# VectorE's reads of kept numbers: an added zero in PSUM, a fixed place in VectorE's order, and a read at every step of the pass to the left

## The chip, the cores and the metric

The kernel runs on one core of one Trainium2 chip. The metric is device time in microseconds (us) from start to end; it is taken as the median of three runs. The core has a matrix engine (TensorE, PE in the profile), VectorE (DVE), ScalarE (ACT), GpSimd (POOL) and SyncE (SP, which issues the DMAs here). Each engine works through a queue of its own in order; an instruction that needs another engine's result waits for a semaphore, and all that is queued behind it on its engine waits too.

## The reference, cut to what matters

The input is `x` of (4, 48, 256, 256) in float32. Four layers follow each other, each `x = x + layer(groupnorm(x))`. Layers 0 and 1 (channel attention and a gated feed-forward) come before the part that is changed. Layers 2 and 3 are alike: recurrent scans over rows, then over columns, each step a five-tap convolution over 48 channels:

```python
def step(w, b):
    def f(carry, inp):
        nxt = inp + _conv1d(carry, w, b)
        return (nxt, nxt)
    return f
...
_, d_rest = jax.lax.scan(step(down_w, down_b), d0, xs[1:])
...
_, u_rest = jax.lax.scan(step(down_w, down_b), u0, seq)
...
_, r_rest = jax.lax.scan(step(right_w, right_b), r0, ws[1:])
...
_, l_rest = jax.lax.scan(step(left_w, left_b), l0, R[Ww - 2::-1])
```

So a layer has four passes, down, up, right and left, of 255 or 256 steps, and each step needs the one before it.

## The kernel before

Layers 2 and 3 are computed in `scans`. The batch of four is split into two chains, 0 and 1, of two images each; a chain goes through layer 2 and then layer 3. The 96 partitions hold 48 channels of even and of odd positions, so a step is two halves (one per image), each of three 96x96 matmuls over 128 positions into one PSUM bank. `step` (L1056) issues for each half the matmuls (L1064; the profile has two records for each float32 matmul, so 12 a step) and VectorE's addition of the PSUM sum and the step's input into the next `carry` (L1068 for down and up, where the input is a row, L1072 for right and left). There are `NC = 4` carry buffers, used in turn. After each addition, `keep` writes the step's result somewhere:

- down and up: ScalarE writes it over the row it came from (`dn`, L1150; `up`, L1194).
- right: ScalarE writes it to `lines` (L1286). The step's input is a column; GpSimd copies it from `col` to a small contiguous tile `pre` (`fetch`, L1259) `far` steps ahead. Chain 0 has three `pre` buffers and `far = 2`; chain 1 has four and `far = 3`.
- left: the input is a line of `lines`, and GpSimd adds the carry to `stage` (L1334), one addition for both halves. In layer 3 of chain 1 (`direct`) it adds each half into `done` (L1338), from where the output is written straight away.

Loads and stores of 1536 KB blocks go over SP's queue: a block is 16 steps in right and left.

An instruction of VectorE that must wait for two engines gets an extra instruction for the second wait. To keep such waits off the additions, VectorE reads now and then one number of what another engine wrote, into a tile `seen` that nobody uses: behind that read, VectorE knows that the other engine has come that far. `look` (L1030) does this in down, up and right: it keeps the place in a list, and reads the place kept three steps before. In right the same instruction reads a number of `pre` for the next step (`fetched`): a `tensor_add` of two SBUF numbers (L1041); otherwise it is a `tensor_copy` (L1039). In left, except in `direct`, a copy (L1348) at every second step reads the place kept two steps before.

A scheduler sets the order of each engine's queue from the program and from its own estimate of when operands are ready. It may place an instruction earlier or later than the program has it, so a `seen` read need not stand where the program asks for it.

The chains are started so that chain 0 goes alone for `LEAD = 992` steps, nearly the whole of its layer 2; then steps of the two chains alternate; then chain 1 does its layer 3 alone, while GpSimd also rearranges the output rows of chain 0 (`to_rows`, L1448). The start of chain 0 overlaps with the end of the gated layer. In left of layer 2, VectorE also takes statistics of the finished block with 8 `bn_stats` of 512 elements (L1376), one a step, for the next group norm.

Of the kernel before, what the change touches and what calls it, by code (L numbers as in the profile page):

```python
# [9 lines left out]
F32 = mybir.dt.float32  # L10
# [3 lines left out]
PSUM = bass.MemoryType.PSUM  # L14
DRAM = bass.MemoryType.DRAM

B, C, H, W = 4, 48, 256, 256
G = 16
NP = 2
P = 96  # L20
# [944 lines left out]
def scans(ctx, tc, xs, out, wts, biases, dram, k, coefs, lead, spare):  # L965
# [13 lines left out]
    nc = tc.nc  # L979
# [3 lines left out]
    pool = lambda name, bufs, **how: ctx.enter_context(  # L983
        tc.tile_pool(name=name, bufs=bufs, reuse_waits="tile", **how)
    )
# [6 lines left out]
    slots_d = pool("c_slot_d", 5)  # L992
    p_small = pool("c_ps", 1, space=PSUM)
    psum = pool("c_psum", 2, space=PSUM)
    sums = [spare, psum]
    buffers = [Ring([slots_a] * 3 + [slots_c, slots_b]), Ring([slots_d] * 5)]
    NT = H // RT
    NH = RT // 2
    CB = 2 * KC
# [16 lines left out]
    def take(pair, name):  # L1016
        return buffers[pair].tile([P, SLOT], F32, tag="slot", name=name)

    def chain(pair):
# [7 lines left out]
        seen = wp.tile([P, 1], F32, tag=f"seen{pair}", name="seen")  # L1027
        kept = []

        def look(place, fetched=None):  # L1030

            kept.append(place)
            if len(kept) > 3:
                if fetched is None:
                    nc.vector.tensor_copy(seen, kept.pop(0))  # L1039
                else:  # L1040
                    nc.vector.tensor_add(seen, kept.pop(0), fetched)  # L1041

        def slot(name):
            return take(pair, f"{name}{pair}")

        def inner():
            return carry[at[0]][:, :, 1 : HP - 1]
# [5 lines left out]
        def blocks(v):  # L1053
            return v.rearrange("p b (k w) -> p b k w", w=KC)
# [30 lines left out]
        def row(ts, r):  # L1085
            return rows_view(ts[r % 2])[:, :, :, r // 2, :]

        def load_rows(layer, n, r, t, k0, k1):

            v = rows_view(t)  # L1090
            for b in range(2):
                for q in range(2):
                    nc.sync.dma_start(
                        v[q * C : (q + 1) * C, b, k0:k1].rearrange("c k h w -> c k (h w)"),
                        xs[layer][pair][
                            r * C : (r + 1) * C, b, 2 * k0 + q : 2 * k1 - 1 + q : 2, n * NH : (n + 1) * NH, :
                        ].rearrange("c k h w -> c k (h w)"),
                    )

        def layer_of(layer, first):  # L1100
# [18 lines left out]
            def norm(t, b):  # L1119
                v = by_batch(t)[:, b]  # L1120
                g = biased[b]
                nc.scalar.activation(v, v, AF.Identity, bias=g[:, 1:2], scale=g[:, 0:1])
# [11 lines left out]
            for n in range(NT):  # L1134
                ahead_ = None
                for r in range(RT):
                    if r == 0:
                        kept.clear()
                        while len(halves) < min(2 * n + 5, 2 * NT):
                            t = slot("dn")  # L1140
                            load_rows(layer, len(halves) // 2, len(halves) % 2, t, 0, NK)
                            halves.append(t)
                        if n + 1 < NT:
                            ahead_ = halves[2 * n + 2 : 2 * n + 4]
                    if ahead_ and r in (11, 14, 22, 25):
                        norm(ahead_[r // 22], r % 11 // 3)
                    inp = row(now, r)

                    def keep(new, b):
                        nc.scalar.activation(inp[:, b], blocks(new[:, b]), AF.Identity, bias=bias[:, 0:1])  # L1150

                    if n == 0 and r == 0:
                        keep(inner(), slice(0, 2))
                    else:
                        step(layer, 0, inp, keep)
                    look(inp[:, 1, 0, 0:1])
                    yield
                if ahead_:
                    for r in range(2):
                        nc.sync.dma_start(D[n][r], now[r])  # L1160
                    now = ahead_
# [90 lines left out]
            fetched = {}  # L1252
# [59 lines left out]
            direct = layer == 1 and pair == NP - 1  # L1312
            done = None
            writes = []
            for n in reversed(range(NK)):
                ahead_ = None
                if direct and n % 2 == 1:
                    done = [take(0, "done") for _ in range(2)]
                for w in reversed(range(CB)):
                    if w == CB - 1 and n > 0:  # L1320
                        ahead_ = slot("lines"), slot("stage")
                        nc.sync.dma_start(ahead_[0], Rt[n - 1])
                        nc.sync.dma_start(by_batch(ahead_[1]), block_of(x, n - 1))
                    if layer == 0 and n == 0 and w == CB // 2:
                        following = [slot("dn"), slot("dn")]
                        for r in range(2):
                            load_rows(1, 0, r, following[r], 1, NK)
                    line = lines_view(lines)[:, w]
                    to = cols_view(stage)[:, :, w % 2, :, w // 2]

                    def keep(new, b):
                        if not direct:
                            if b.stop == 2:
                                nc.gpsimd.tensor_add(to, to, new)  # L1334
                            return
                        for i in range(b.start, b.stop):
                            place = done[i].rearrange("p (h w) -> p h w", w=2 * CB)[:, :, n % 2 * CB + w]
                            nc.gpsimd.tensor_add(place, to[:, i], new[:, i])  # L1338

                    if n == NK - 1 and w == CB - 1:  # L1340
                        keep(inner(), slice(0, 2))
                    else:
                        step(layer, 2, line, keep)
                    if not direct and w % 2:

                        kept.append(to[:, 1, H // 2 - 1 :])
                        if len(kept) > 1:
                            nc.vector.tensor_copy(seen, kept.pop(0))  # L1348
                    if late:
                        late.pop(0)()  # L1350
                    if writes and w % 8 == 4:
                        writes.pop(0)()
                    yield
                if layer == 0:
                    nc.sync.dma_start(block_of(y, n), by_batch(stage))
                elif not direct:
                    v = stage.rearrange("p (b q t n) -> p b q t n", b=2, q=2, t=NY)
                    for b in range(2):
                        for q in range(2):
                            nc.sync.dma_start(result[:, b, :, 2 * n + q], v[:, b, q])  # L1360
                elif n % 2 == 0:

                    def write(b, r, done=done, w0=n * CB):
                        at_rows = out[(2 * pair + b) * C : (2 * pair + b + 1) * C].rearrange(
                            "c (h r w) -> c h r w", r=2, w=W
                        )
                        nc.sync.dma_start(
                            at_rows[:, :, r, w0 : w0 + 2 * CB],
                            done[b][r * C : (r + 1) * C].rearrange("c (h w) -> c h w", w=2 * CB),
                        )  # L1370

                    writes += [lambda b=b, r=r, f=write: f(b, r) for b in range(2) for r in range(2)]
                if layer == 0:

                    def stat(b, c, n=n, v=by_batch(stage)):
                        nc.vector.bn_stats(stats[b][:, n * 4 + c, :], v[:, b, c * 512 : (c + 1) * 512])  # L1376

                    late += [lambda b=b, c=c, f=stat: f(b, c) for b in range(2) for c in range(4)]
                    if n == 0:
                        for r in range(2):  # L1380
                            for q in range(2):
                                nc.sync.dma_start(
                                    rows_view(following[r])[q * C : (q + 1) * C, :, 0].rearrange("c b h w -> c b (h w)"),
                                    cols_view(stage)[r * C : (r + 1) * C, :, q, :NH, :].rearrange("c b h w -> c b (h w)"),
                                )
                if ahead_:
                    lines, stage = ahead_
# [211 lines left out]
```

## Time and profile before

| | us |
|---|---|
| median of three runs | 9099.63 |
| the three runs | 9097.15 to 9100.62 |
| the profiled execution, its own time | 9105.24 |
| its span, first to last instruction | 9103.5 |
| PE busy | 8713.5 (96% of the span) |
| DVE busy | 3971.3 (44%) |
| ACT busy | 3440.2 (38%) |
| POOL busy | 1948.2 (21%) |
| scan matmuls, L1064: first start to last start | 3247.2 to 9070.5 |

The reads and additions on VectorE, by line, from the groups of instructions (line, engine, operation, out<-in, size, count, then busy us and mean ns of one, then idle time of the engine before them and what ended it):

```profile
L1072 DVE TENSOR_TENSOR carry<-ps,pre 96x128 f32<-96x128 f32 x2040 | 550.9, 284 | 271.1 <-PE ps L1064 239.7
...
L1041 DVE TENSOR_TENSOR seen<-lines,pre 96x1 f32<-96x1 f32 x1008 | 166.8, 165 | 479.6 <-POOL pre L1259 437.2
```

Where the chains are, by the first and last times of the lines: chain 0's down and up from 3247 to 4186, its right from 4186 to 4580, its left from 4580 to about 4980; both chains until about 7600; chain 1 alone after that, its last right from 8365 to 8715 and its last left from 8715 to 9071. A timeline line reads: start, duration, engine, line, operation, tiles, count, and in brackets how long the engine had been idle and who released it. A line of the table by stages reads: from and to, length, busy time and in brackets the number of records, the granted clock as a share of full speed, the busy share of the DMA engines, GB/s.

### The profile page before, as it was taken

What the parts mean: (1) busy time and instruction counts of PE and PEld (TensorE: products, weight loads), DVE (VectorE), ACT (ScalarE), POOL (GpSimd) and SP (SyncE); (2) the same over time, 40 slices, a digit from 0 to 9 for tenths busy, and PEclk for the clock granted to TensorE, in tenths of its full rate; (3) what the DMA queues carried; (4) which work ended last, traced back from release to release, by engine and by line L of the source; (5) the groups of instructions that cost most, each with busy time, mean ns of one, the idle gap of its engine ahead of it and who ended that gap; (6) DMA issues with size and microseconds to landing.
All of it is one profiled execution on the core that took longest, in us unless ns stands there. A gap on an engine that the chain in (4) does not pass through costs nothing. (4 is left out here: it accounts for less than half of the span.)

```text
span 9103.5 us, 158554 instructions
## 1 busy us (share of the span) xinstructions
PE 8713.5 (96%) x62920; PEld 7234.4 (79%) x62920; DVE 3971.3 (44%) x14031; ACT 3440.2 (38%) x7023; POOL 1948.2 (21%) x3100
## 2 busy tenths in 40 slices
PE   6999999999999978999999999999999999999998
PEld 4777777433333336999888999999999999999998
DVE  3232010234555555444345544444444555444543
ACT  0011000123343455765400776666554002765610
POOL 0000000001111120002444000001445664001566
PEclk9999999999999988999999999999999999999999
DMA  7664323467878877765466755465556787867789
GB/s 150 132 133 89 71 62 73 94 137 168 180 171 179 180 159 163 161 143 143 119 168 165 168 140 135 116 152 134 161 158 163 215 224 175 204 168 191 210 171 184
DMA packets 1180201, 1390.37 MB, mean 153 GB/s; under 512 B 263184, under 2 KB 1107216, under 8 KB 1118784
## 3 DMA queue, kind: packets, MB, share of 16 engines
q1 hardware_dynamic: 1179360, 1379.90, 64.9%
q8 instruction: 493, 8.08, 0.4%
q14 instruction: 252, 2.06, 0.1%
q0 software_dynamic: 96, 0.33, 0.0%
HBM read 811.21 MB, written 509.61 MB: 145 GB/s over the span
## 5 line engine op out<-in xcount | busy, mean ns | idle before, releaser
L1064 PE MATMUL ps<-carry,w 96*96 96x128 f32 x48960 | 5490.2, 274 | 115.0 <-DVE carry L1072 71.7
L1064 PEld LDWEIGHTS ps<-carry,w 96*96 96x96 f32 x48960 | 5407.4, 163 | 207.4 <-DVE carry L1072 134.7
L1259 POOL COPY pre<-col 96x256 f32<-96x256 f32 x1020 | 656.7, 644 | 2755.5 <-DMA col<-last 1971.7
L1150 ACT ACTIVATE dn<-carry,b 96x128 f32<-96x128 f32 (+1 forms) x2044 | 769.1, 398 | 838.3 <-DVE carry L1068 828.9
L1286 ACT ACTIVATE lines<-carry,b 96x128 f32<-96x128 f32 (+1 forms) x2044 | 780.2, 399 | 690.8 <-DVE carry L1072 650.1
L1068 DVE TENSOR_TENSOR carry<-ps,dn 96x128 f32<-96x128 f32 x2280 | 652.5, 287 | 755.8 <-PE ps L1064 730.5
L1194 ACT ACTIVATE up<-carry,b 96x128 f32<-96x128 f32 x1792 | 719.1, 402 | 459.8 <-DVE carry L1068 456.3
L1068 DVE TENSOR_TENSOR carry<-ps,up 96x128 f32<-96x128 f32 x1792 | 516.0, 288 | 598.9 <-PE ps L1064 594.1
L1334 POOL TENSOR_TENSOR stage<-stage,carry 96x256 f32<-96x256 f32 x768 | 656.2, 856 | 527.4 <-DVE carry L1072 497.5
L1072 DVE TENSOR_TENSOR carry<-ps,lines 96x128 f32<-96x128 f32 x2040 | 547.6, 283 | 424.9 <-PE ps L1064 401.1
L581 PE MATMUL py<-x1n,wy 128*96 128x512 f32 x1536 | 703.6, 607 | 30.4 <-ACT x1n L541 27.9
L1072 DVE TENSOR_TENSOR carry<-ps,pre 96x128 f32<-96x128 f32 x2040 | 550.9, 284 | 271.1 <-PE ps L1064 239.7
L295 PE MATMUL acc<-xs,xt 128*96 128x288 f32 x2048 | 666.7, 407 | 0.0
L294 PE MATMUL acc<-xt 128*96 128x288 f32 x2048 | 666.5, 409 | 0.0
L581 PEld LDWEIGHTS py<-x1n,wy 128*96 128x96 f32 x1536 | 245.2, 166 | 455.2 <-issue 437.0
L279 DVE COPY xt<-pt 128x384 f32<-128x384 f32 x256 | 136.6, 554 | 850.8 <-PE pt L276 650.3
L261 ACT ACTIVATE xn<-raw,coef 96x2048 f32<-96x2048 f32 x64 | 133.6, 2094 | 987.6 <-PE pt L276 819.6
L296 PE MATMUL acc<-xt,xs 128*96 128x192 f32 x2048 | 501.7, 327 | 0.0
L296 PEld LDWEIGHTS acc<-xt,xs 128*96 128x96 f32 x2048 | 332.1, 165 | 154.3 <-issue 1.4
L295 PEld LDWEIGHTS acc<-xs,xt 128*96 128x96 f32 x2048 | 332.0, 164 | 151.2 <-issue 2.2
L604 DVE TENSOR_TENSOR y<-py,t 96x512 f32<-96x512 f32 x256 | 171.4, 678 | 600.8 <-PE py L590 600.8
L1041 DVE TENSOR_TENSOR seen<-lines,pre 96x1 f32<-96x1 f32 x1008 | 166.8, 165 | 479.6 <-POOL pre L1259 437.2
(183 smaller groups left out, 5520.3 us busy)
## 6 DMA issues: line engine op xcount, KB each, us to landing
stage<-x SPq DMA_DIRECT2D x64, 1536.0 KB
dn<-x SPq DMA_DIRECT2D x240, 384.0 KB
R<-lines SPq DMA_DIRECT2D x60, 1536.0 KB
lines<-R SPq DMA_DIRECT2D x60, 1536.0 KB
D<-dn SPq DMA_DIRECT2D x56, 1536.0 KB
up<-D SPq DMA_DIRECT2D x56, 1536.0 KB
U<-up SPq DMA_DIRECT2D x224, 384.0 KB
col<-U SPq DMA_DIRECT2D x56, 1536.0 KB
```

Of the source, the lines that this page charges most:

```text
L294: nc.tensor.matmul(acc[0], lhsT=xt[:, h + 2, :], rhs=xt[:, here, :], start=first, stop=last)
L295: nc.tensor.matmul(acc[1], lhsT=xt[:, h + 2, :], rhs=xs[:, here, :], start=first, stop=last)
L296: nc.tensor.matmul(acc[2], lhsT=xs[:, h + 2, :], rhs=xt[:, past, :], start=first, stop=last)
L581: nc.tensor.matmul(ps, lhsT=held["w"][0][:, dx], rhs=x1n[:, 2 * c : 2 * c + 2, dx : dx + W], start=dx == 0, stop=False)
L1064: nc.tensor.matmul(ps, lhsT=w_sb[layer][:, way, j, :], rhs=old[:, i, j : j + W // 2], start=j == 0, stop=j == 2)
L1068: nc.vector.tensor_add(new[:, i].rearrange("p (k w) -> p k w", w=KC), ps.rearrange("p (k w) -> p k w", w=KC), inp[:, i])
L1072: nc.vector.tensor_add(new[:, i], ps, inp[:, i])
L1150: nc.scalar.activation(inp[:, b], blocks(new[:, b]), AF.Identity, bias=bias[:, 0:1])
L1194: nc.scalar.activation(place[:, b], blocks(new[:, b]), AF.Identity, bias=bias[:, 1:2])
L1259: nc.gpsimd.tensor_copy(t, cols_view(block)[:, :, w % 2, :, w // 2])
L1286: nc.scalar.activation(line[:, b], new[:, b], AF.Identity, bias=bias[:, 2:3])
L1334: nc.gpsimd.tensor_add(to, to, new)
```

## The change

A PSUM tile `zero` of one number per partition is allocated in `scans` and set to 0.0 by VectorE once. Every read is now a `tensor_add` of this zero and the number to be read. In right, the kept place and the fetched number are read by two instructions instead of one, and the fetched number is read at every step, also while the list is still short. Each read is pinned by `keep_in_program_order`: in VectorE's queue it stands behind the VectorE instruction that the program traced just before it, normally the step's second addition; it is not a wait. Later instructions may still be put ahead of it. Chain 0 leaves out the reads in the first 64 rows of down in layer 2. In left, `look` is called at every step and in `direct` too (on `done` there), and so reads the place kept three steps before.

```diff
+    p_zero = pool("c_zero", 1, space=PSUM)
     sums = [spare, psum]
+    zero = p_zero.tile([P, 1], F32, tag="zero", name="zero")
+    nc.vector.memset(zero, 0.0)
...
             kept.append(place)
-            if len(kept) > 3:
-                if fetched is None:
-                    nc.vector.tensor_copy(seen, kept.pop(0))
-                else:
-                    nc.vector.tensor_add(seen, kept.pop(0), fetched)
+            old = [kept.pop(0)] if len(kept) > 3 else []
+            for number in old + ([] if fetched is None else [fetched]):
+                tc.keep_in_program_order(nc.vector.tensor_add(seen, zero, number))
...
                         step(layer, 0, inp, keep)
-                    look(inp[:, 1, 0, 0:1])
+                    if pair or layer or n > 1:
+
+                        look(inp[:, 1, 0, 0:1])
                     yield
...
                         step(layer, 2, line, keep)
-                    if not direct and w % 2:
-
-                        kept.append(to[:, 1, H // 2 - 1 :])
-                        if len(kept) > 1:
-                            nc.vector.tensor_copy(seen, kept.pop(0))
+                    if direct:
+                        look(done[1].rearrange("p (h w) -> p h w", w=2 * CB)[:, 0, n % 2 * CB + w : n % 2 * CB + w + 1])
+                    else:
+                        look(to[:, 1, 0:1])
                     if late:
                         late.pop(0)()
```

## The prediction

> **What bounds the kernel now.** I read the page first. TensorE is busy 96% of the span and VectorE 44%, so this is a TensorE kernel; the question is where TensorE pauses. Busy time hides short pauses (a matmul record lasts 270 ns, while a new one starts about every 109 ns), so I used the table by stages for the scan's matmuls (line 1064) and counted records:
>
> ```profile
> core 0: us, PE busy (x), PEclk, DMA share, GB/s
> ...
> 3880.00:4186.00 306.00, 306.00 (x2797) 1.00 0.61 141
> 4186.00:4580.00 394.00, 371.08 (x3060) 1.00 0.51 138
> 4580.00:4980.00 400.00, 364.44 (x3068) 1.00 0.60 166
> 5300.00:6200.00 900.00, 900.00 (x8229) 1.00 0.56 135
> ...
> 8365.00:8715.00 350.00, 340.35 (x3053) 0.99 0.72 199
> 8715.00:9071.00 356.00, 349.50 (x3069) 0.99 1.00 186
> ```
>
> 900 us for 8229 records is 109.37 ns each at full rate; a step has 12 records, 1.312 us. What each stage takes beyond that: chain 0 alone going right (4186 to 4580) 394 - 3060 x 0.10937 = 59.3 us; chain 0 going left (4580 to 4980) 400 - 335.5 = 64.5 us; chain 1 alone going right (8365 to 8715) 16.1 us; chain 1 going left (8715 to 9071) 20.3 us. The stage up (3880 to 4186) and the long stretch with both chains lose almost nothing. So nearly all that a change on VectorE can win is in these four stages. Who is waited for, from VectorE's waits in 4186 to 4980:
>
> ```profile
> DVE seen L1041 <- POOL pre L1259: 199.1, 247, 1.1
> DVE carry L1072 <- PE ps L1064: 131.8, 304, 0.9
> DVE seen L1348 <- POOL stage L1334: 95.1, 121, 1.0
> ```
>
> The kept numbers' reads (`seen`), not the additions, wait for GpSimd. VectorE's timeline shows what that does, first at a step of right:
>
> ```profile
> 4400.78 0.16 DVE L1041 TENSOR_TENSOR seen<-lines,pre 96x1 f32<-96x1 f32 x1 [0.81 <-POOL pre L1259]
> 4400.86 0.28 DVE L1072 TENSOR_TENSOR carry<-ps,pre 96x128 f32<-96x128 f32 x1
> 4401.41 0.29 DVE L1072 TENSOR_TENSOR carry<-ps,pre 96x128 f32<-96x128 f32 x1 [0.28 <-PE ps L1064]
> 4402.50 0.15 DVE L1041 TENSOR_TENSOR seen<-lines,pre 96x1 f32<-96x1 f32 x1 [0.81 <-POOL pre L1259]
> ```
>
> The read stands ahead of the step's two additions. In the queue as built it reads the `pre` of two steps ahead, although the program asks for the next step's: the scheduler let it float one step forward. Chain 0 has three `pre` buffers, so that copy starts only when the step just finished has released its buffer. Hence: second addition ends at 4401.70, copy 4401.83 to 4402.47, read 4402.50, and only then the addition. Against this, a healthy step of up:
>
> ```profile
> 3900.91 0.29 DVE L1068 TENSOR_TENSOR carry<-ps,up 96x128 f32<-96x128 f32 x1 [0.37 <-PE ps L1064]
> 3901.12 0.14 DVE L1039 COPY seen<-up 96x1 f32<-96x1 f32 x1
> 3901.57 0.29 DVE L1068 TENSOR_TENSOR carry<-ps,up 96x128 f32<-96x128 f32 x1 [0.31 <-PE ps L1064]
> ```
>
> The read lies in the gap between the second addition and the next step's first: the following instruction can start at 3901.12 and the addition is due at 3901.57, so 0.45 us are free.
>
> [...] a read that takes 0.16 us elsewhere takes 1.03 us beside a 1.12 us copy:
>
> ```profile
> 8561.07 1.12 POOL L1448 COPY oo<-oi 96x1024 f32<-96x1024 f32 x1
> 8561.16 1.03 DVE L1041 TENSOR_TENSOR seen<-lines,pre 96x1 f32<-96x1 f32 x1 [0.15 <-POOL pre L1259]
> ```
>
> [...]
>
> **Part by part.** Sums are against the profiled execution: span 9103.5 us, 9105.2 us with what lies around it, 5.6 us above the median of the runs, 9099.6. I subtract from the median.
>
> *Pinning, right.* In the changed queue a step reads: first addition, second addition, read of the line three steps old, read of the next step's `pre`. That `pre` was released by the addition two steps back, so it is finished over a step before. The wait goes. What must fit is two reads instead of one in the 0.45 us. An addition with a PSUM input takes 286 ns for 128 elements[...]. The second read waits for the first to finish (both write `seen`); the nearest such pair is L604 and L605, where the next one starts 0.04 us after the end. So 0.02 + 0.154 + 0.04 + 0.02, then 0.08 until the addition may start behind a read (4400.78 to 4400.86): 0.31 of 0.45 us. It fits. Bounds: 0.20 at least, for two reads that overlap; 0.55 if each takes its whole duration and as much again for its wait, 0.10 too late. I take 0.31. Of chain 0's 59.3 us I leave the few pauses over 0.5 us at block boundaries (about 3): gain 56. In chain 1's right the zero in PSUM ends the 1.03 us reads; of the 16.1 us one wait of 6.5 us at its start (TensorE for `carry` of L1290) belongs to the turn; I count 6.
>
> *Left, chain 0.* Now every second step's read waits for GpSimd's 0.86 us `stage` addition of a step too recent. Afterwards a read at every step asks for the one three steps back; that is done, since GpSimd needs 0.86 of 1.31 us. It demands nothing new: the next step's addition overwrites the carry which that same GpSimd addition read. But the 64.5 us are not all the reads'. Each block of 16 steps also has 8 `bn_stats` of 0.68 us, 0.60 apart (L1376). In before they alternate with additions: first additions at 4711.03, 4712.88, 4714.85, 4716.43, 4717.94 are 6.91 us for 4 steps instead of 5.25, a loss of 1.67. In the changed queue they stand one, two, two, two, one behind the step's read: two of them push the next first addition from +0.66 to +1.50 us behind the second addition. Following the steps (an addition opens its half's next matmuls 0.34 us after its start, these take 0.656, the next addition starts 0.31 later), first additions come at 0.26, 1.81, 3.72, 5.42, 7.19, 8.50 instead of 6.82 at the fifth: 1.7 again. So about 15 x 1.67 = 25 us stay, and the gain is 40. If a block's statistics cost 1 us more or less, this moves 15 us.
>
> *Left, chain 1, layer 1.* Before has no reads there; each addition carries its wait for GpSimd, and a step takes 356/255.75 = 1.392 us. Reads would free TensorE, but the DMA share is 1.00 from 8715 to 9071 and 0.81 until 9104, and the last writes are issued from 9039 to 9096. Faster steps wait for DMA: 0, with 10 as upper bound.
>
> *Small edits with one answer.* The memset of zero is one instruction near the gated layer's end, off the path. Dropping chain 0's reads in its first 64 rows removes some 58 copies which pile up behind the gated layer's last statistics (3553 to 3573): 2. In the two-chain stretch 1590 more reads (in the whole program) of 0.15 us on an engine half idle cost nothing: each chain's addition has the other's step, 1.31 us, as cover; pauses at 6200 to 7600 (about 8 us) should shrink by 3. Some 120 additions in chain-alone down and up stages get an extra 21 ns wait instruction, about 3 us lost.
>
> Sum: 56 + 6 + 40 + 0 + 2 + 3 - 3 = 104. 9099.6 - 104 = 8996.
>
> **Rivals.**
> 1. *The two reads do not quite fit in right*: 0.10 late in 510 single-chain steps is 51 us: 9047. For: the chained wait on VectorE's own result is new and TensorE has no slack at all in a single chain[...]. Against: 0.14 us margin.
> 2. *Left does not recover*: statistics placed in pairs, or blocks bound by the loads (a write takes some 12 us before `lines` may be loaded), keep its 64 us: 9036. Against: the DMA share there is 0.60, and both-chains left runs at 220 GB/s and loses 4 us in 500.
> 3. *Slower*: each read with its chained wait takes x; the right step is late by 2x - 0.45. To eat the 104 us and 18 more (0.2%, about what a measurement of this kernel tells from no change) over 510 steps it must be 0.24 late, x = 0.345 us, twice the sum above; at x = 0.36 it is 0.27 late, 138 us: 9134. Nothing in the trace is near.
>
> **How the numbers follow.** Forecast 0.72, rival 1 0.11, rival 2 0.07, rival 3 0.08, and 0.02 for gains and losses that cancel. The forecast's own spread: best case 59 + 8 + 50 + 10 + 8 = 135, so 8965; worst, with two thirds of right and left, about 9030. The range takes in both first rivals: 8962 to 9047. Faster 0.89, within 0.2% 0.03, slower 0.08.
>
> **What would show it.** Right: chain 0's 255 steps in about 337 us, `seen` waiting for `pre` near zero. Left: no `seen` waiting 0.97 us for `stage`, `bn_stats` in pairs, blocks of about 24 us instead of 26.5. No `seen` over 0.3 us. The tail from chain 1's left on as long as before. I am wrong if first additions of right start later than 0.66 us behind the second ones, or if left's blocks stay at 26 us.

## The result, and the profile after

The changed kernel takes 8976.43 us (median of four runs, 8971.29 to 8983.88); the kernel before took 9100.12 us beside it. The ratio is 0.9865, 95% interval 0.9848 to 0.9882: 124 us less, where 104 had been forecast. The profiled execution has a span of 8982.1 us, against 9103.5.

Stage by stage, each stage measured from the first addition of one pass to the first addition of the next (us, from the profiled executions; "turn" is the passage from one layer of a chain to the next):

| | before | after | difference |
|---|---|---|---|
| start of chain 0's right | 4186.4 | 4182.5 | -3.9 |
| chain 0's right | 395.0 | 335.5 | -59.5 |
| from chain 0's left to chain 1's last right | 3790.3 | 3738.9 | -51.4 |
| chain 1's last right | 345.1 | 337.8 | -7.3 |
| chain 1's last left | 354.1 | 355.0 | +0.9 |
| from its last addition to the end | 32.6 | 32.3 | -0.3 |

The start of chain 0's right lay between 4170 and 4189 us in the twelve kernels of this study, with no pattern that follows the edits, so the -3.9 is no finding. Of the long third row, the starts of the scan's matmul records tell where TensorE paused (every distance over 0.125 us, less the 0.109 us that a record takes at full rate): 64.9 us before and 23.8 after in the first 400 us of chain 0's left; 8.8 and 4.7 in the 190 us that follow, with its turn into layer 3; 3.8 and 0.8 in the 1700 us with both chains that follow later; 14.7 and 8.1 in the 600 us in which both chains go left; 16.3 and 18.6 in the 585 us up to chain 1's last right. Stretches of 3 to 10 us in which the granted clock stood at half count among these pauses: in the one from 4916.4 in the kernel after, 6.8 us at a clock of 0.50, the records follow at 0.213 us (median of 29).

The table by stages of the kernel after, for the scan's matmuls (L1064 is now L1067), columns as before:

```profile
core 0: us, PE busy (x), PEclk, DMA share, GB/s
3880.00:4181.00 301.00, 301.00 (x2747) 1.00 0.60 140
4181.00:4517.00 336.00, 335.78 (x3062) 1.00 0.60 160
4517.00:4917.00 400.00, 388.58 (x3445) 1.00 0.71 191
8253.00:8594.00 341.00, 338.75 (x3062) 0.99 0.74 204
8594.00:8950.00 356.00, 345.30 (x3060) 0.97 1.01 185
```

Right of chain 0 (second row) is 336 us for 3062 records, 109.7 ns each: TensorE now goes at full rate there. Left of chain 0 (third row) has 3445 records in 400 us, where before had 3068. Chain 1's last left (last row) still takes 356 us with the DMA engines busy all the time.

VectorE's waits from 4181 to 4980 (waited for, us in total, times, longest):

```profile
DVE carry L1075 <- PE ps L1067: 214.6, 620, 0.7
DVE carry L1071 <- PE ps L1067: 36.2, 93, 1.1
DVE st L1380 <- POOL stage L1339: 18.6, 30, 0.9
```

The 199 us for `pre` and the 95 us for `stage` on the `seen` reads are gone. VectorE waits for TensorE instead, which is what should be in a kernel that TensorE bounds; the only wait for GpSimd left is that of the statistics (`st`, `bn_stats`). VectorE's timeline at a step of right:

```profile
4401.46 0.29 DVE L1075 TENSOR_TENSOR carry<-ps,pre 96x128 f32<-96x128 f32 x1 [0.37 <-PE ps L1067]
4401.66 0.14 DVE L1044 TENSOR_TENSOR seen<-zero,lines 96x1 f32<-96x1 f32 x1
4401.91 0.15 DVE L1044 TENSOR_TENSOR seen<-zero,pre 96x1 f32<-96x1 f32 x1
4402.11 0.29 DVE L1075 TENSOR_TENSOR carry<-ps,pre 96x128 f32<-96x128 f32 x1
```

Second addition, read of the line at +0.20, read of `pre` at +0.45, next first addition at +0.65: the distance that TensorE asks for. And in left, around the end of a block:

```profile
4701.39 0.15 DVE L1044 TENSOR_TENSOR seen<-zero,stage 96x1 f32<-96x1 f32 x1
4702.44 0.69 DVE L1380 BATCH_NORM_STATS2 st<-stage 96x6 f32<-96x512 f32 x1 [0.90 <-POOL stage L1339]
4703.05 0.47 DVE L1075 TENSOR_TENSOR carry<-ps,lines 96x128 f32<-96x128 f32 x2
...
4705.48 0.14 DVE L1044 TENSOR_TENSOR seen<-zero,stage 96x1 f32<-96x1 f32 x1
4705.55 1.27 DVE L1380 BATCH_NORM_STATS2 st<-stage 96x6 f32<-96x512 f32 x2
4706.74 0.56 DVE L1075 TENSOR_TENSOR carry<-ps,lines 96x128 f32<-96x128 f32 x2
```

Reads wait for nothing. The first statistic of the block stands ahead of the next step's additions and waits 0.90 us for GpSimd's last `stage` addition of that block; later ones stand in pairs of 1.27 us, and the next additions come in twos (x2, no idle time before them): they were ready and had to wait. TensorE pauses 1.33 us at this block's end, 0.72 of it behind the first statistic and 0.61 behind the pairs. The prediction left a loss here in its sum, but put it down to the pairs alone.

### The profile page after: what moved, and what is told of

It reads as the page before. It is cut to its first block, busy times and chain, and to the rows that moved or that the text cites. A ratio compares the mean times of both kernels' runs of the same rounds, so it can differ in the third digit from the quotient of the medians.

```text
span 8982.1 us, 162711 instructions
## 1 busy us (share of the span) xinstructions
PE 8646.3 (96%) x62920; PEld 7223.1 (80%) x62920; DVE 4167.5 (46%) x15625; ACT 3479.8 (39%) x7023; POOL 1948.9 (22%) x3100
## 5 line engine op out<-in xcount | busy, mean ns | idle before, releaser
L1067 PE MATMUL ps<-carry,w 96*96 96x128 f32 x48960 | 5423.7, 273 | 59.3 <-DVE carry L1071 29.1
L1067 PEld LDWEIGHTS ps<-carry,w 96*96 96x96 f32 x48960 | 5397.6, 163 | 95.0 <-issue 44.9
L1291 ACT ACTIVATE lines<-carry,b 96x128 f32<-96x128 f32 (+1 forms) x2044 | 819.8, 402 | 583.9 <-DVE carry L1075 574.0
L1075 DVE TENSOR_TENSOR carry<-ps,lines 96x128 f32<-96x128 f32 x2040 | 576.8, 286 | 562.8 <-PE ps L1067 552.9
L1075 DVE TENSOR_TENSOR carry<-ps,pre 96x128 f32<-96x128 f32 x2040 | 586.7, 288 | 457.6 <-PE ps L1067 402.4
L590 PE MATMUL py<-x2n,wy 64*96 64x512 f32 x1536 | 363.0, 601 | 0.0
```

The lines of the kernel that those rows point to most:

```text
L1067: nc.tensor.matmul(ps, lhsT=w_sb[layer][:, way, j, :], rhs=old[:, i, j : j + W // 2], start=j == 0, stop=j == 2)
L1075: nc.vector.tensor_add(new[:, i], ps, inp[:, i])
L1291: nc.scalar.activation(line[:, b], new[:, b], AF.Identity, bias=bias[:, 2:3])
```

## The experiments

Two questions stood open: which part of the edit brings the gain (the place in VectorE's order, the zero in PSUM, the split reads, a read at every step of left), and what is lost still in left. Ten kernels were run. A table first; the stage columns are as above, in us, from the profiled executions, and each ratio is to runs of the kernel before that were taken beside that kernel (their medians lie between 9092 and 9100 us):

| kernel | median, us | ratio to before, 95% interval | chain 0's right | chain 0's left to chain 1's last right | chain 1's last right | last left and end |
|---|---|---|---|---|---|---|
| before | 9100.12 | | 395.0 | 3790.3 | 345.1 | 386.7 |
| after | 8976.43 | 0.9865 [0.9848, 0.9882] | 335.5 | 3738.9 | 337.8 | 387.3 |
| e1_pin_only | 8978.54 | 0.9870 [0.9855, 0.9885] | 337.0 | 3737.5 | 338.9 | 387.1 |
| e11_zero_only | 9090.59 | 0.9998 [0.9989, 1.0007] | 394.9 | 3789.5 | 344.2 | 388.6 |
| e2_no_pin | 9183.19 | 1.0094 [1.0077, 1.0111] | 394.8 | 3871.0 | 344.2 | 395.3 |
| e3_left_as_before | 9021.80 | 0.9917 [0.9903, 0.9932] | 336.2 | 3785.7 | 338.2 | 387.6 |
| e6_copy | 8972.29 | 0.9863 [0.9848, 0.9877] | 335.8 | 3734.2 | 338.0 | 387.2 |
| e7_reads_twice | 8984.43 | 0.9876 [0.9862, 0.9891] | 341.1 | 3736.1 | 343.8 | 387.6 |
| e9_stats_half | 8971.16 | 0.9862 [0.9847, 0.9876] | 335.5 | 3725.8 | 338.4 | 387.6 |
| e10_pin_half_stats | 8971.60 | 0.9864 [0.9848, 0.9881] | 335.2 | 3723.6 | 339.1 | 385.8 |
| e8_stats_pinned | 8948.12 | 0.9838 [0.9821, 0.9854] | 335.5 | 3708.8 | 338.1 | 387.6 |
| e14_pin_stats512 | 8955.04 | 0.9845 [0.9830, 0.9860] | 337.0 | 3711.5 | 339.2 | 389.4 |

The order of VectorE's queue, as it stands in four of the built programs (`a`, `b`: the two additions of chain 0's step; `s`: read of a kept place of ScalarE; `p`: read of `pre`, in before with a kept line in one instruction; `S`: read of `stage`; `N`: one `bn_stats`; `x`, `y`: additions of chain 1), and what is read behind the additions of a step t:

```
                 right         p reads     left, with the end of a block     S reads
before           abpabpabpabp  pre of t+3  aSNbNaNbNaSxbyasbSababSababSabab  stage of t
after            abspabspabsp  pre of t+1  abSNNabSNaxybSabSabSabSabSabSabS  stage of t-3
e2_no_pin        asbpasbpasbp  pre of t+3  aSNbSNaSNbNaSxbyaSbSabSabSabSabS  stage of t
e8_stats_pinned  abspabspabsp  pre of t+1  abSNaybSNabSNabSNabSNabSNaxbSabS  stage of t-3
```

The letters stand nearly alike; what differs is of which step the number is. Not pinned, a read of `pre` stands two steps ahead of its place in the program (the prediction counted one), and a read of `stage` two or three: it asks for an addition of GpSimd that can start only now.

### The place in the order alone

The kernel before, whose three old reads are pinned where they are; still two SBUF inputs in right, a copy at every second step in left, none in chain 1's last left.

```diff
-                    nc.vector.tensor_copy(seen, kept.pop(0))
+                    tc.keep_in_program_order(nc.vector.tensor_copy(seen, kept.pop(0)))
...
-                    nc.vector.tensor_add(seen, kept.pop(0), fetched)
+                    tc.keep_in_program_order(nc.vector.tensor_add(seen, kept.pop(0), fetched))
...
-                            nc.vector.tensor_copy(seen, kept.pop(0))
+                            tc.keep_in_program_order(nc.vector.tensor_copy(seen, kept.pop(0)))
```

> The kernel before with one thing changed: its reads, as they are (copies, and in right one addition of two SBUF numbers; every second step in left, none in direct), are pinned behind the step's additions. Theory (the place in the queue is what counts): chain 0's right falls from 395.0 us to about 336, its left (200 steps from its start) from 331.5 to about 297, chain 1's right stays near 345 because its reads still hold two SBUF inputs beside GpSimd's copies; total about 9002. Rival (the zero in PSUM is what counts[...]): no stage moves by more than 10 us, total 9085 to 9100.

It gives 8978.54 us, where 9002 was expected, and a ratio of 0.9870, not to be told from the whole change's 0.9865; and stage by stage nearly the same times: the first 200 steps of chain 0's left take 294.9 us (before 331.5, after 294.2). Chain 1's last right is the surprise: 338.9 us, nearly all of its gain, although its reads still meet GpSimd's copy of output rows. The timeline of this kernel there:

```profile
8471.55 0.29 DVE L1072 TENSOR_TENSOR carry<-ps,pre 96x128 f32<-96x128 f32 x1 [0.28 <-PE ps L1064]
8471.60 1.14 POOL L1448 COPY oo<-oi 96x1024 f32<-96x1024 f32 x1
8471.76 0.98 DVE L1041 TENSOR_TENSOR seen<-lines,pre 96x1 f32<-96x1 f32 x1
8472.66 0.55 DVE L1072 TENSOR_TENSOR carry<-ps,pre 96x128 f32<-96x128 f32 x2
```

The read takes 0.98 us and the next addition starts 1.11 us behind the second one instead of 0.66: 0.45 us late. Few reads fall upon such a copy: in the kernel before 10 of the 252 of this pass, at 0.64 to 1.04 us; of its other reads two take 0.47 and 0.48, the rest 0.16 at most. Over the pass this kernel is 338.9 - 337.8 = 1.1 us behind the whole change, which is the most that reads with two SBUF inputs can cost here; the zero itself isn't needed to save it, for pinned copies, with one SBUF input, take 338.0 (e6 below).

### The zero and the split reads alone

The kernel before with the added zero and with two reads in right, nothing pinned, left as before. (Chain 0 leaves out the reads in its first 64 rows here too; the kernel with the pin alone above kept them, so they are not what the gain comes from.)

```diff
+            old = [kept.pop(0)] if len(kept) > 3 else []
+            for number in old + ([] if fetched is None else [fetched]):
+                nc.vector.tensor_add(seen, zero, number)
```

> The kernel before with the zero in PSUM and right's two separate reads only: no pinning, left as before. Theory (order is all): chain 0's right stays near 395, left near 331 for 200 steps, chain 1's right within 2 us of 345; total 9085 to 9100. It also tells whether it was the unpinned read at every step of left that made the unpinned version slower than before (then this one is not slower), or the split reads in right (then this one is near 9180 too). Rival [...]: chain 1's right falls by 6 us or more and the total by more than 10.

0.9998 with an interval on both sides of 1. The groups of instructions (us busy, mean ns, then idle time before them and who ended it) of this kernel and of the pinned one:

```profile
L1044 DVE TENSOR_TENSOR seen<-zero,pre 96x1 f32<-96x1 f32 x1020 | 157.0, 154 | 446.8 <-POOL pre L1264 410.9
```

```profile
L1041 DVE TENSOR_TENSOR seen<-lines,pre 96x1 f32<-96x1 f32 x1008 | 166.0, 165 | 3.7 <-DVE carry L1072 3.7
```

With the zero, the reads of `pre` in chain 1's last right take 157 ns at most, so the meeting with GpSimd's copy no longer lengthens them; the 411 us of waiting for `pre` in the whole program stay, since the read still asks for the `pre` of t+3. In chain 1's last right itself the zero does shorten the waits for `pre`, from 30.6 us to 8.2, but the pass by only 0.9 us: what remains are a few long waits at the head of VectorE's queue, where GpSimd does copies of output rows before the copy to `pre`:

```profile
8471.58 2.18 POOL L1453 COPY oo<-oi 96x1024 f32<-96x1024 f32 x2
8473.70 0.63 POOL L1264 COPY pre<-col 96x256 f32<-96x256 f32 x1
8474.36 0.15 DVE L1044 TENSOR_TENSOR seen<-zero,pre 96x1 f32<-96x1 f32 x1 [1.47 <-POOL pre L1264]
```

TensorE pauses 1.1 us there. With the pin, reads are as long as ever and wait for nothing. The place is the cause, not the operands.

### The change without its pin

```diff
-                tc.keep_in_program_order(nc.vector.tensor_add(seen, zero, number))
+                nc.vector.tensor_add(seen, zero, number)
```

> The changed kernel without the pinning; zero in PSUM and the reads at every step of left stay. In its queue a right step reads the pre of two steps ahead again, ahead of the first addition. Theory: chain 0's right goes back to 395 us or a little more (a second read now stands between the two additions), left keeps its gain because the read there stands between the two additions where the wait for GpSimd is over in time; total about 9035. Rival (the zero counts): right stays at 336, total about 8976.

1.0094: slower than before by 86 us. Right is back at 394.8 us; that was expected. That left would keep its gain was expected too, and it was wrong: the loss sits where the reads of left now stand at every step and float: VectorE's waits from 7000 to 7700, and its timeline with both chains going left:

```profile
DVE seen L1044 <- POOL stage L1339: 345.7, 370, 1.4
```

```profile
7300.36 0.15 DVE L1044 TENSOR_TENSOR seen<-zero,stage 96x1 f32<-96x1 f32 x1 [0.97 <-POOL stage L1339]
7300.43 0.47 DVE L1075 TENSOR_TENSOR carry<-ps,lines 96x128 f32<-96x128 f32 x2
7301.88 0.15 DVE L1044 TENSOR_TENSOR seen<-zero,stage 96x1 f32<-96x1 f32 x1 [0.97 <-POOL stage L1339]
7301.95 0.47 DVE L1075 TENSOR_TENSOR carry<-ps,lines 96x128 f32<-96x128 f32 x2
```

Each read asks for the `stage` addition of the step just finished, and waits 0.97 us for it; the other chain's additions stand behind the read, so the second chain is no cover, and steps follow at 1.52 us in place of 1.31. In the kernel before the same stretch had 219 such waits (191.5 us), with a read at every second step. So a read at every step is harmless only in its fixed place.

### Left as before

The whole change, but for left, which has its old copy at every second step, not pinned.

> The changed kernel with left as before: an unpinned copy at every second step of the place two steps back, none in direct. Theory: chain 0's left takes 331 us for 200 steps again instead of 294, all else stays (chain 1's last left at 355 us with or without reads); total about 8976 + 42 = 9018. Rival [...]: the copy of one number costs little, left stays below 305, total below 8990.

9021.8 us, where 9018 was expected: 45 us of the gain go, and by the table 3785.7 - 3738.9 = 46.8 of them lie between chain 0's left and chain 1's last right. Chain 1's last left, here without any read, takes with its end 387.6 us; with a read at every step 387.3.

### A copy in place of the addition of a zero

```diff
-                tc.keep_in_program_order(nc.vector.tensor_add(seen, zero, number))
+                tc.keep_in_program_order(nc.vector.tensor_copy(seen, number))
```

> The changed kernel with tensor_copy of the number in place of the addition of the zero: same places, all pinned, no PSUM operand. Theory (the zero does nothing for the time): all stages within 2 us of the changed kernel, total 8970 to 8985. Rival [...]: chain 1's right rises from 338 towards 345, total above 8985.

0.9863: no difference that these runs can tell. A pinned copy does what the pinned addition does.

### Each read of right twice

This asks how much room is left behind the additions: four reads a step, in the order line, `pre`, line, `pre`.

```diff
-            for number in old + ([] if fetched is None else [fetched]):
+            for number in (old + ([] if fetched is None else [fetched])) * (1 if fetched is None else 2):
```

> The changed kernel with both of right's reads done twice, so that three of them stand between the second addition and the next step's first (the fourth between the two additions). It prices a chained read. Theory: each read waits for the one before and they follow at 0.25 us (measured in the changed kernel); the third starts 0.70 after the second addition, the addition 0.08 later, 0.12 too late; through the matmuls that costs 0.06 us a step where a chain runs alone: chain 0's right from 335.5 to about 351, chain 1's from 338 to about 353, nothing while both run; total about 9007. Rival (pinned reads overlap the additions and cost nothing on this path): right stays at 336 and 338, total 8976.

Right takes 5.6 us longer in chain 0 and 6.0 in chain 1, about 0.022 us a step; about 15 had been expected. The scheduler put the fourth read between the two additions, so three lie in the gap. Its timeline:

```profile
4400.83 0.29 DVE L1075 TENSOR_TENSOR carry<-ps,pre 96x128 f32<-96x128 f32 x1 [0.27 <-PE ps L1067]
4401.04 0.14 DVE L1044 TENSOR_TENSOR seen<-zero,lines 96x1 f32<-96x1 f32 x1
4401.29 0.15 DVE L1044 TENSOR_TENSOR seen<-zero,pre 96x1 f32<-96x1 f32 x1
4401.48 0.15 DVE L1044 TENSOR_TENSOR seen<-zero,lines 96x1 f32<-96x1 f32 x1
4401.55 0.28 DVE L1075 TENSOR_TENSOR carry<-ps,pre 96x128 f32<-96x128 f32 x1
```

The third read follows 0.19 us behind the second, and the addition comes at +0.72 instead of +0.65. Three reads are some 0.07 us too many, so two have about 0.12 us to spare (an estimate, 0.19 less 0.07). Most of the 0.07 us does not reach the step's length: in chain 0's right the first addition comes 0.72 us behind the second one (median), and the second then 0.60 behind the first, in place of 0.66.

### The statistics of left, smaller and one a step

16 statistics of 256 columns for each block instead of 8 of 512, each pinned behind its step's read; e9 on the kernel after, e10 on the kernel before with pinned reads.

```diff
-                stats = [wp.tile([P, NK * 4, 6], F32, tag=f"st{pair}{b}", name="st") for b in range(2)]
+                stats = [wp.tile([P, NK * 8, 6], F32, tag=f"st{pair}{b}", name="st") for b in range(2)]
...
-                        nc.vector.bn_stats(stats[b][:, n * 4 + c, :], v[:, b, c * 512 : (c + 1) * 512])
+                        tc.keep_in_program_order(nc.vector.bn_stats(stats[b][:, n * 8 + c, :], v[:, b, c * 256 : (c + 1) * 256]))
```

> The changed kernel, with left's statistics in 16 pieces of 256 elements a block, one a step, pinned behind the step's read, instead of 8 of 512 that the queue holds in pairs. Theory: what is left over in chain 0's left (294.2 us for 200 steps instead of 262.4) are the pairs: [...] read and piece fit in the 0.45 us between additions; 200 steps take about 275 (chain 1's single steps are among them), total about 8960. Rival (the leftover is waiting for GpSimd or loads at the block's turn, or a piece does not fit and delays every step): 294 or more, total 8976 or above.

> A combination: the kernel before with its reads pinned as they are, and left's statistics in 16 pinned pieces of 256 elements a block. Theory: pinning and the spread statistics add up, without the zero, the split reads or reads at every step of left: chain 0's left at full rate (200 steps in 263), its right about 337; total about 8970, like the changed kernel with the spread statistics (8971). Rival (with a read at only every second step the statistics meet late reads): left 275 or more, total 8978 or above.

In e9 TensorE then pauses 0.6 us from 4515 to 4905, where it pauses 19.7 in the kernel after, so the statistics were what left still lost. A statistic of 256 columns takes 0.41 us there, and the addition behind it starts 0.38 after it (4700.73 to 4701.11), on time at +0.65. The first 200 steps of left take 263.0 us, and 262.6 in e10. But the times are 8971.16 and 8971.60 us, no clear step below the whole change. In the profiled executions e9 is 13.1 us shorter in the third row and starts chain 0's right 6.9 us later than the kernel after; since e10, with the same larger tile, starts only 0.2 us later, the larger tile does not explain that. What the third row fails to gain lies at the turns. Half as wide statistics are twice as many to put together at the layer's end. Two lines of e9 at that turn, of VectorE's and of TensorE's timeline, and the same operation in the kernel after:

```profile
4906.05 3.61 DVE L1400 BATCH_NORM_AGGREGATE mv<-st 96x2 f32<-96x768 f32 x1
```

```profile
4909.71 0.33 PE L88 MATMUL pg<-mv,cst 96*96 96x1 f32 x2 [2.60 <-DVE mv L1400]
```

```profile
4912.98 1.87 DVE L1400 BATCH_NORM_AGGREGATE mv<-st 96x2 f32<-96x384 f32 x1
```

TensorE stands 2.6 us for each of the two that a turn has; in the kernel after it stands 0.9 us in all. In the 591 us of chain 0's left and turn together e9 pauses 12.7 us (28.5 in the kernel after), nearly all of it at the turn: 5.2 us are these two waits, and some 5 us more come from two stretches, 3.4 us from 4910.6 and 6.8 us from 4924.3, in which the granted clock stood at half. They lie at the two waits, but whether the waits bring them is not shown: the kernel after has such a stretch at this turn and e6, with the same wait of 0.9 us, has none. In the 600 us where both chains go left, with chain 1's turn, e9 pauses 11.5 us (8.1 after). What left gains is in part given back at the turns.

### The statistics as they are, one a step

The same pin for the 8 statistics of 512 columns; e8 on the kernel after, e14 on the kernel before with pinned reads.

```diff
-                        nc.vector.bn_stats(stats[b][:, n * 4 + c, :], v[:, b, c * 512 : (c + 1) * 512])
+                        tc.keep_in_program_order(nc.vector.bn_stats(stats[b][:, n * 4 + c, :], v[:, b, c * 512 : (c + 1) * 512]))
```

> The kernel after, with left's 15 statistics of 512 columns each pinned as the only extra VectorE instruction of a step (no bigger tile). If what left still loses is a pair of statistics ahead of one step's addition, the loss of a block of 16 steps falls from about 1.2 us to what one statistic of 0.6 us beside a read costs a step: if it fits, left gains some 13 us and, with no change of memory, the gated layer keeps its overlap: 8963 us. If one statistic with the read is already longer than the step's free time, each step of left is 0.1 to 0.3 us late and the time is 8976 or above, up to 9020.

> The kernel before with its old reads pinned, and left's statistics of 512 columns pinned one a step as in the other run. Left's copy stands in every second step only, so more room beside the statistic. If the statistic fits: 8963 us, as the other or a little under. If it doesn't: between 8976 and 9000, less late than the other since only half of the steps have a copy too.

Both lie below what was expected: 8948.12 us (8943.55 to 8951.86) and 8955.04 us (8943.25 to 8958.82); e14 is 23.5 us below e1, its own starting point. The longest run of e8 is 19 us below the shortest of the kernel after; as ratios to before, 0.9838 [0.9821, 0.9854] and 0.9865 [0.9848, 0.9882] still overlap a little. The place of the gain is plain: 3738.9 - 3708.8 = 30 us between chain 0's left and chain 1's last right. VectorE's timeline in e8, two steps of left with a statistic:

```profile
4711.10 0.15 DVE L1044 TENSOR_TENSOR seen<-zero,stage 96x1 f32<-96x1 f32 x1
4711.16 0.68 DVE L1380 BATCH_NORM_STATS2 st<-stage 96x6 f32<-96x512 f32 x1
4711.76 0.27 DVE L1075 TENSOR_TENSOR carry<-ps,lines 96x128 f32<-96x128 f32 x1
4712.20 0.29 DVE L1075 TENSOR_TENSOR carry<-ps,lines 96x128 f32<-96x128 f32 x1 [0.17 <-PE ps L1067]
```

The read and one statistic do not fit into the gap, for which 8976 us or more had been expected: the second addition of that step starts at 4710.89, so the first of the next comes at +0.87, 0.21 us late. Two such steps take 2.84 us (4711.76 to 4714.60) in place of 2.62. Yet TensorE does not pause: from 4520 to 4821 no two of its scan records are more than 0.125 us apart. What it does in the 0.22 us is shown by its own queue, as it stands in the built programs (`A`, `B`: the three matmuls of a half of chain 0's step; `X`: one matmul of chain 1, two records or 0.22 us):

```
                 TensorE's queue in left, at the end of a block
after            BXXABXXABXXABABABAB
e8_stats_pinned  BABABXABABXABABXABABXAB
```

Chain 1's first steps are spread over chain 0's left, and at every second step one matmul of theirs stands ahead of the matmuls that need the late addition. The lateness is covered with work that had to be done anyway. What a statistic beside the read would cost a chain that has no other to cover it, no run shows. In the kernel after a pair of statistics is too much for such a cover: the second addition at 4705.27 (0.29 before its group's end) is followed by the next first one at 4706.74, 1.47 us later and 0.81 late, and two `X` are 0.44 us.

TensorE pauses 5.5 us in the 591 us of left and turn, against 28.5, and 3.7 in the 600 us with both chains left, against 8.1. Not all of this is the statistics' doing. The kernel after had the granted clock at half for 6.8 us at each of these two turns (from 4916.4 and from 7500.2), e8 at neither; at 0.213 us a record in place of 0.109, each such stretch costs TensorE about half its length, an estimate of 3.4 us. So the placing of the statistics in the kernel after costs about 28.5 - 5.5 - 3.4, by estimate some 20 us, in chain 0's left and turn. Of the 30 us between the two kernels in the third row, 10 are time at half clock (36 us of it in the kernel after, 16 in e8); over the twelve kernels this loss in the row lies between 8 and 20 us, and no run shows that the pin lowers it.

## Why the prediction was right, and where it was not

- **Right of chain 0**: forecast -56, measured -59.5. The chained second read was put at 0.31 us of a free 0.45, margin 0.14; the 0.154 us in it for the read itself was the author's estimate, and the read of `pre` with the zero takes 154 ns (median, e11). The runs show 0.25 us from the first read to the second, 0.20 from the second to the addition, exactly at TensorE's pace, and, by the estimate from e7, about 0.12 us to spare. Rivals 1 and 3, which let the two reads be too long, fall with that. That the unpinned read had floated one step forward was miscounted: it is two (it reads the `pre` of t+3); the wait that follows was read rightly. The 3 us kept back for pauses at the blocks' ends were not there.
- **Chain 1's last right**: forecast -6, measured -7.3, and here the step was wrong although its number is near, by luck. The prediction gave the 6 us to "the zero in PSUM ends the 1.03 us reads", the author's estimate, which no run had shown by then. The zero without the place ended those reads (157 ns at most in e11) and brought 0.9 us (345.1 to 344.2); the place without the zero brought 6.2 with reads up to 0.98 us still there. What cost time was the wait at the head of the queue, as in chain 0: where the place was left as it was and the long reads ended, waits of up to 1.5 us for `pre` remained. That a read is long says nothing of its price; what stands behind it, and when that is due, does.
- **Left of chain 0**: forecast -40, measured -41 in TensorE's pauses of the 400 us that the forecast looked at (64.9 to 23.8), and 4 more in the turn that follows, which it had left out. The term that stays, 15 blocks by 1.67 us = 25 us for the statistics, measured about 20 (19.7 us of pauses in the kernel after from 4515 to 4905). The placing in twos was read rightly from the queue; two things were left out, the first statistic's wait for GpSimd, behind which more than half of a block's loss lies, and chain 1's matmuls, which cover a part. (The additions that it counts as first ones in the kernel before, from 4711.03 on, are second ones by the queue; their distance, and so the 1.67, is the same.) Rival 2 (left does not recover) falls: GpSimd's addition of three steps back is done whenever it is asked for (no read waits for `stage` from 4181 to 4980). A read at every step was not needed for it: e1's copies at every second step bring the same (294.9 against 294.2 us for 200 steps).
- **Chain 1's last left**: forecast 0, on the reading that the DMA engines bound it (share 1.00 in the kernel before). Measured 387.3 us to the end, with reads; 387.6 without, at a DMA share of 1.01. The reads in `direct` bring nothing and cost nothing where they are pinned; unpinned, as in e2, pass and end took 395.3.
- **With both chains**: forecast -3, measured about -7 (3.8 to 0.8, 14.7 to 8.1, 16.3 to 18.6). The stretch in which both chains go left was under-sized: the other chain's step was taken as cover, but its additions stand behind the waiting read in the same queue, and of the 191.5 us of waits there not all were hidden.
- **Small terms**: -2 for the gated layer's end and +3 for additional wait instructions (21 ns each, median; in the kernel before 800 stand with the 1008 reads of L1041, 511 with the 512 additions of L1072 from 8715 to 9071, where no reads stand, and 100 with its 3568 others) cannot be told apart from the spread of 4170 to 4189 us in the start of right.

So 59.5 + 51.4 + 7.3 and some 3 us in the small rows make the 121 us of the profiled executions. The forecast of 104 was short by several small amounts: about 3.5 us in chain 0's right, 4 at its turn, 4 with both chains, 1.3 in chain 1's last right, and the 3 us set aside for wait instructions, of which nothing can be seen. Its rival of a slower kernel priced the wrong danger: not the length of a chained read, but a read at every step that is free to float, which e2 shows at 86 us.

## What to carry to other kernels

An instruction whose only purpose is to absorb a wait must have a place in the queue where the waited-for result is already there; where a scheduler may move it, see where it ended up, and fix it before changing its operands. The same question is worth asking of other small instructions on that engine: one pinned line on the statistics brought 25 to 28 us more (by the ratios and by the medians), of which some 20, by the estimate above, come from its place; the zero, the split and the additional reads brought nothing that can be measured. Spread such work evenly, one piece for each step, and see in the waiting engine's queue whether it has other work to cover the small delays; cutting the pieces finer lengthened what is done once at the end.

## What was not expected of the hardware

- A one-number read on VectorE behind another that writes the same tile follows at 0.25 us when it is the second of its step (247 of 252 in chain 0's right after), and at 0.19 us when it is the third (251 of 252 in e7); each by itself takes 0.14 to 0.15 us. An addition that depends on neither starts 0.07 us behind the last read where TensorE is already done (4401.48 to 4401.55 in e7).
- A one-number read beside a GpSimd copy of 1.14 us takes up to 0.98 us with two SBUF inputs (e1) and, with a zero in PSUM as one of them, at most 155 ns (24 reads beside such copies in chain 1's last right of the kernel after); over a pass of 255 steps with such copies this was worth 1.1 us at most.
- `bn_aggr` takes 1.87 us for 384 numbers in a partition (after) and 3.61 us for 768 (e9), nearly twice as long for twice the numbers; `bn_stats` takes 0.68 us for 512 columns (after) and 0.41 for 256 (e9).
- An addition 0.21 us late did not make TensorE pause where its queue held one matmul of the other chain (0.22 us) at that point (e8).
